# Layer norm's centring and max with zero: from VectorE to ScalarE, with the negated mean as bias

## The chip, the cores and the metric

The kernel runs on one core of a Trainium2 chip. The metric is device time in microseconds (us), the median of the runs. The core's engines are TensorE (PE; PEld is its load of the stationary operand), VectorE (DVE), ScalarE (ACT), GpSimd (POOL) and SyncE (SP, which here only issues DMAs). Each has its own queue of instructions [...].

## The reference, cut to what matters

Four graph attention layers with a residual, on x of 16 graphs, 1024 nodes and 256 features, f32:

```
for layer in 0..3:
    h = maximum(layernorm(x), 0)           # per node: (x - mean) / sqrt(var + eps), eps 1e-5
    x = x + gat_layer(h, adj, W, a)        # Wh = h @ W; masked softmax-like weights; weights @ Wh
```

The layers differ in the form of their weights (leaky ReLU, ReLU, its negative) and in what follows the sum (nothing, ELU, ELU, four heads with a norm of their own). Since the reciprocal root is positive, it may be applied after the projection: `max(x - mean, 0) @ W`, then times rstd.

## The kernel before, in words

One program, unrolled over the 16 graphs (`batch(b)`). Two streams, one for even and one for odd graphs, are written as Python generators; a small loop always advances the stream with the smaller sum of yielded costs, so that the text of the program alternates between two graphs in different layers. The instructions of an engine then stand in an order that a planner makes from this text and the dependencies. It need not be the order of the text: in the trace, L226 of a layer norm stands between L273 and L274 of another tile's finish.

`project(l, xb, pair, evict)` is the function that the diff touches. It handles two tiles of 128 nodes ("a pair"; 4 pairs x 4 layers x 16 graphs = 256 calls, called a project below):

- VectorE: `bn_stats` (L220) and `bn_aggr` (L221) for each of the two rows of tiles, mean and variance in `mv`
- VectorE L211 and GpSimd L212: `rstd`
- VectorE L226, twice: `above` = max(x - mean, 0), 128 x 256
- TensorE L230: two transposes of each `above` into the PSUM tile `turned` (named misc, 3 buffers)
- ScalarE L232: copy of `turned` to `hT` in SBUF
- TensorE L236: `projected` = hT x W, 4 matmuls for each row of tiles
- `evict`: ScalarE's exponentials (L286, L306) and a scaled copy to `V` or `h` (VectorE L290, ScalarE L288 and L307), in layer 3 also GpSimd (L309, L313, L314; L314 adds a constant to x in place)

`weigh` makes the attention weights: ScalarE copies a row from PSUM (L251), and VectorE multiplies it with the mask, 8 times 128 x 512 (L255), for each half of the target nodes. `attend` multiplies the weights with V (TensorE L338, `acc`), and a finish puts the result into x: in layer 0 on VectorE alone (L263, L264, L354), in layers 1 and 2 with the ELU (`add_elu`: VectorE L263, L264, L273, L274, ScalarE L271 `below`, GpSimd L275). In layer 3 the matmul is L414, ScalarE copies its result to `sums` (L418), TensorE transposes that (L423), and VectorE, GpSimd and ScalarE norm the heads. `load` fetches a graph to come: ScalarE squares and casts its adjacency tiles (L116, L122).

After finish(i) for even i, `attend` calls `project` of the next layer for the two rows of tiles just done, so the layer norm follows the end of the layer before, tile by tile. The tiles named `above` come from the pool `work` with 3 buffers, shared by `project` and `add_elu`; `mv` and other small tiles have 6.

Of the kernel before, what the change touches and what calls it, by code (L numbers as in the profile page):

```python
# [31 lines left out]
F32 = mybir.dt.float32  # L32
# [4 lines left out]
AF = mybir.ActivationFunctionType  # L37
ALU = mybir.AluOpType
AX = mybir.AxisListType

P = 128
# [17 lines left out]
def short_path(ctx: ExitStack, tc: tile.TileContext, ins: dict, out: bass.AP, bad: bass.AP):  # L59

    nc = tc.nc
# [72 lines left out]
    bias = const.tile([P, D], F32, name="bias")  # L134
# [11 lines left out]
    with tc.tile_pool(name="prep", bufs=2) as prep:  # L146
# [30 lines left out]
        for l, form in enumerate(forms):  # L177
            n = EXT[l] // 3
# [25 lines left out]
    small = ctx.enter_context(tc.tile_pool(name="small", bufs=6))  # L204
# [4 lines left out]
    def inverse_root(var: bass.AP, n: int, eps: float, scale: float = 1.0) -> bass.AP:  # L209
        r = small.tile([P, n], F32, name=f"rstd{n}")  # L210
        nc.vector.tensor_scalar(r, var, scale, eps, op0=ALU.mult, op1=ALU.add)  # L211
        nc.gpsimd.tensor_tensor(r, r, minus_half.to_broadcast([P, n]), op=ALU.pow)  # L212
        return r

    def project(l: int, xb: bass.AP, pair: int, evict):

        mv = small.tile([P, 2, nc.vector.BN_AGGR_DIM], F32, name="mv")
        for n in range(2):
            stats = small.tile([P, nc.vector.BN_STATS_DIM], F32, name="stats")
            nc.vector.bn_stats(stats, xb[:, 2 * pair + n, :])  # L220
            nc.vector.bn_aggr(mv[:, n, :], stats)  # L221
        rstd = inverse_root(mv[:, :, 1], 2, LN_EPS)
        turned = psum.tile([P, NK, 2 * P], F32, name="misc", bufs=3)
        for n in range(2):
            above = work.tile([P, D], F32, name="above")
            nc.vector.tensor_scalar(  # L226
                above, xb[:, 2 * pair + n, :], mv[:, n, 0:1], 0.0, op0=ALU.subtract, op1=ALU.max
            )
            for k in range(NK):
                nc.tensor.transpose(turned[:, k, ts(n, P)], above[:, ts(k, P)], ident)  # L230
        hT = wide.tile([P, NK, 2 * P], F32, name="hT")
        nc.scalar.copy(hT, turned)  # L232
        for n in range(2):
            projected = psum.tile([P, D + EXT[l]], F32, name="projected")
            for k in range(NK):
                nc.tensor.matmul(  # L236
                    projected, hT[:, k, ts(n, P)], W[l][:, k, :],
                    start=(k == 0), stop=(k == NK - 1),
                )
            evict(2 * pair + n, projected, rstd[:, n : n + 1])  # L240
# [36 lines left out]
    def batch(b: int):  # L277
# [40 lines left out]
        def attend(l: int, V: bass.AP, finish, then: int):  # L318
# [12 lines left out]
            for i in range(NI):  # L331
                t = next(weighing[1], None)
                if t:
                    yield t
                acc = psum.tile([P, HALF], F32, name="acc", bufs=3)[:, : D + 1]
                w = halves[i // NG]
                for j in range(NI):
                    nc.tensor.matmul(  # L338
                        acc, w[:, j, ts(i % NG, P)], V[:, j, : D + 1],
                        start=(j == 0), stop=(j == NI - 1),  # L340
                    )
                finish(i, acc)
                yield 3.6
                if i % 2 == 0 and i > 0:
                    project(then, xb, i // 2 - 1, following[1])
                    yield 4.0
            project(then, xb, NI // 2 - 1, following[1])
            yield 4.0
            return following[0]
# [12 lines left out]
        for pair in range(NI // 2):  # L362
            project(0, xb, pair, evict)
            yield 4.0
# [473 lines left out]
```

## Time and profile before

| | |
|---|---|
| median of 3 runs | 3343.65 us (3341.39 to 3344.26) |
| the profiled execution | 3342.89 us |
| its span, first to last instruction | 3341.3 us |
| granted TensorE clock | 0.988 of full |
| TensorE busy | 3103.0 us, 93% |
| VectorE busy | 2504.0 us, 75% |
| ScalarE busy | 974.3 us, 29% |
| GpSimd busy | 1091.2 us, 33% |

A group in the profile is a line of the kernel on one engine: how many instructions, their busy time together, the mean of one in ns, then the idle time of the engine directly before them and what ended it. The chain is followed back from the last instruction: each step to what released it, or to the instruction before it on its engine. A wait is an engine's idle time before an instruction, put down to the producer that came last.

### The profile page before, as it was taken

What the parts mean: (1) busy time and instruction counts of PE and PEld (TensorE: products, weight loads), DVE (VectorE), ACT (ScalarE), POOL (GpSimd) and SP (SyncE); (2) the same over time, 40 slices, a digit from 0 to 9 for tenths busy, and PEclk for the clock granted to TensorE, in tenths of its full rate; (3) what the DMA queues carried; (4) which work ended last, traced back from release to release, by engine and by line L of the source; (5) the groups of instructions that cost most, each with busy time, mean ns of one, the idle gap of its engine ahead of it and who ended that gap; (6) DMA issues with size and microseconds to landing.
All of it is one profiled execution on the core that took longest, in us unless ns stands there. A gap on an engine that the chain in (4) does not pass through costs nothing.

```text
span 3341.3 us, 38569 instructions
## 1 busy us (share of the span) xinstructions
PE 3103.0 (93%) x13702; PEld 2107.8 (63%) x13702; DVE 2504.0 (75%) x6140; ACT 974.3 (29%) x2081; POOL 1091.2 (33%) x1286
## 2 busy tenths in 40 slices
PE   6899999999989999899998999989999899998987
PEld 5765756657656675665756667566666666656652
DVE  5677787777778777787777877778777787777766
ACT  3423323232232322323233232332323223232121
POOL 1223324233242332424234142242323423234242
PEclk9999999999999999999999999999999999999998
DMA  4101101011010110101011010010101101000000
GB/s 115 26 4 16 32 11 40 7 17 29 13 39 8 16 29 13 38 10 16 26 16 35 10 42 4 13 35 13 39 4 17 32 13 38 7 10 13 1 13 14
DMA packets 55192, 73.19 MB, mean 22 GB/s; under 512 B 4049, under 2 KB 37969, under 8 KB 54993
## 3 DMA queue, kind: packets, MB, share of 16 engines
q0 software_dynamic: 18432, 33.56, 6.7%
q1 hardware_dynamic: 36560, 37.10, 3.5%
q8 instruction: 110, 1.80, 0.2%
q14 instruction: 90, 0.73, 0.1%
HBM read 87.43 MB, written 16.78 MB: 31 GB/s over the span
## 4 chain that ended last, share of the span: by engine, by line
DVE 45%; PE 42%; POOL 5%; ACT 4%; issue 3%; DMA 1%; SPq 0%; ACTq 0%; POOLq 0%; DVEq 0%
DVE weights L255 25%; PE acc L338 18%; PE acc L414 11%; PE projected L236 10%; DVE above L226 3%; PE misc L230 3%; DVE above L273 2%; DVE stats L220 2%; DVE above L274 2%; POOL x_b L275 2%; DVE V L290 2%; DVE y L380 1%; POOL y L379 1%; POOL rstd L212 1%; ACT below L271 1%
## 5 line engine op out<-in xcount | busy, mean ns | idle before, releaser
L338 PE MATMUL acc<-V,weights 128*128 128x257 f32 x6144 | 1454.9, 385 | 12.5 <-DVE weights L255 11.5
L338 PEld LDWEIGHTS acc<-V,weights 128*128 128x128 f32 x6144 | 1137.8, 191 | 208.9 <-DVE weights L255 47.2
L414 PE MATMUL acc<-weights,V 128*65 128x512 f32 x2048 | 914.2, 593 | 0.3 <-DVE weights L255 0.3
L255 DVE SCALAR_TENSOR_TENSOR weights<-row,ex,mask 128x512 f32<-128x512 f32 x1024 | 762.7, 784 | 2.7 <-ACT row L251 0.9
L255 DVE SCALAR_TENSOR_TENSOR weights<-row,V,mask 128x512 f32<-128x512 f32 x768 | 559.4, 776 | 53.0 <-ACT row L251 52.9
L414 PEld LDWEIGHTS acc<-weights,V 128*65 128x65 f32 x2048 | 278.7, 138 | 492.7 <-issue 474.0
L212 POOL TENSOR_TENSOR rstd<-rstd,minus_half 128x2 f32<-128x2 f32 (+1 forms) x320 | 311.3, 975 | 745.7 <-DVE rstd L211 703.2
L236 PE MATMUL projected<-W,hT 128*128 128x259 f32 (+1 forms) x2048 | 521.8, 398 | 14.8 <-ACT hT L232 11.3
L236 PEld LDWEIGHTS projected<-W,hT 128*128 128x128 f32 x2048 | 383.5, 195 | 130.1 <-ACT hT L232 60.4
L275 POOL TENSOR_TENSOR x_b<-x_b,above 128x256 f32<-128x256 f32 x256 | 227.5, 890 | 585.8 <-DVE above L274 532.5
L230 PE MATMUL misc<-ident,above 128*128 128x128 f32 x1024 | 189.1, 289 | 155.3 <-DVE above L226 108.6
L271 ACT ACTIVATE below<-acc,inv 128x256 f32<-128x256 f32 x256 | 120.0, 472 | 607.4 <-DVE inv L264 497.0
L232 ACT COPY hT<-misc 128x512 f32<-128x512 f32 x256 | 149.1, 586 | 495.8 <-PE misc L230 494.8
L230 PEld LDWEIGHTS misc<-ident,above 128*128 128x128 f32 x1024 | 113.7, 143 | 256.0 <-DVE above L226 120.3
L220 DVE BATCH_NORM_STATS2 stats<-x_b 128x6 f32<-128x256 f32 x512 | 206.7, 414 | 83.1 <-POOL x_b L275 78.9
L263 DVE TENSOR_SCALAR inv<-acc 128x1 f32<-128x1 f32 x256 | 37.3, 150 | 272.5 <-PE acc L338 272.3
L418 ACT COPY sums<-acc 65x512 f32<-65x512 f32 x128 | 74.0, 578 | 546.2 <-PE acc L414 546.1
L226 DVE TENSOR_SCALAR above<-x_b,mv 128x256 f32<-128x256 f32 x512 | 222.0, 443 | 3.8 <-POOL x_b L275 1.7
L105 POOL DMA_DIRECT2D adj_i<-in_adj_dram x128 | 77.1, 603 | 406.3 <-ACT sums L418 174.4
L290 DVE TENSOR_SCALAR V<-projected,rstd,V 128x256 f32<-128x256 f32 x256 | 134.8, 537 | 63.9 <-ACT V L286 62.9
L286 ACT ACTIVATE V<-projected,rstd 128x3 f32<-128x3 f32 x384 | 99.4, 261 | 262.0 <-PE projected L236 220.1
L314 POOL TENSOR_TENSOR x_b<-x_b,beta 128x256 f32<-128x256 f32 x128 | 117.3, 923 | 150.7 <-DVE above L226 148.6
(70 smaller groups left out, 2370.1 us busy)
## 6 DMA issues: line engine op xcount, KB each, us to landing
adj_i<-in_adj_dram POOLq DMA_DIRECT2D x128, 256.0 KB, 3.8
x_b<-in_x_dram SPq DMA_DIRECT2D x16, 1024.0 KB, 7.8
out_dram<-y SPq DMA_DIRECT2D x32, 512.0 KB, 3.8
W<-in_L_gnn_W_dram SPq DMA_DIRECT2D x3, 256.0 KB, 3.0
a_b<-in_L_gnn_a_dram SPq DMA_DIRECT2D x3, 256.0 KB, 6.4
a_b<-in_L_gnn_a_src_dram SPq DMA_DIRECT2D x1, 640.0 KB, 7.5
a_b<-in_L_gnn_a_dst_dram SPq DMA_DIRECT2D x1, 640.0 KB, 9.4
W<-in_L_gnn_W_dram SPq DMA_DIRECT2D x2, 128.0 KB, 8.9
```

The source lines that it names most:

```text
L212: nc.gpsimd.tensor_tensor(r, r, minus_half.to_broadcast([P, n]), op=ALU.pow)
L220: nc.vector.bn_stats(stats, xb[:, 2 * pair + n, :])
L226: nc.vector.tensor_scalar(above, xb[:, 2 * pair + n, :], mv[:, n, 0:1], 0.0, op0=ALU.subtract, op1=ALU.max)
L230: nc.tensor.transpose(turned[:, k, ts(n, P)], above[:, ts(k, P)], ident)
L232: nc.scalar.copy(hT, turned)
L236: nc.tensor.matmul(projected, hT[:, k, ts(n, P)], W[l][:, k, :], start=(k == 0), stop=(k == NK - 1),)
L255: nc.vector.scalar_tensor_tensor(w[:, j, :], r, c(j), mask[:, j, ts(half, HALF)], op0=op, op1=ALU.mult)
L271: nc.scalar.activation(below, acc[:, :D], AF.Exp, scale=inv)
L275: nc.gpsimd.tensor_add(xi, xi, above)
L290: nc.vector.tensor_scalar(V[:, i, :D], projected[:, :D], rstd, V[:, i, D : D + 1], op0=ALU.mult, op1=ALU.mult,)
L338: nc.tensor.matmul(acc, w[:, j, ts(i % NG, P)], V[:, j, : D + 1], start=(j == 0), stop=(j == NI - 1),)
L414: nc.tensor.matmul(accT, V3[:, j, h, :], w[:, j, :], start=(j == 0), stop=(j == NI - 1))
```

## The change

Behind the statistics of the two rows of tiles ScalarE makes `minus_mean`, 128 x 2, from both means. Then, for each row of tiles, ScalarE writes `above` as Relu(x + minus_mean) with `minus_mean`'s column as bias per partition, instead of VectorE's tensor_scalar (subtract, then max with 0). `minus_mean` is a new small tile with 6 buffers; the transposes read `above` as before. `inverse_root` stays on VectorE and GpSimd. All other lines are unchanged; the planner makes the order of each engine anew.

```diff
         rstd = inverse_root(mv[:, :, 1], 2, LN_EPS)
+        minus_mean = small.tile([P, 2], F32, name="minus_mean")
+        nc.scalar.mul(minus_mean, mv[:, :, 0], -1.0)
         turned = psum.tile([P, NK, 2 * P], F32, name="misc", bufs=3)
         for n in range(2):
             above = work.tile([P, D], F32, name="above")
-            nc.vector.tensor_scalar(
-                above, xb[:, 2 * pair + n, :], mv[:, n, 0:1], 0.0, op0=ALU.subtract, op1=ALU.max
+            nc.scalar.activation(
+                above, xb[:, 2 * pair + n, :], AF.Relu, bias=minus_mean[:, n : n + 1]
             )
```

## The prediction

> **What bounds the kernel now.** I read the page first (busy shares, the shares of the chain, the costly groups), then the sum of the waits, then the chain in order of time, then the timeline around a few layer norms.
>
> From the page, and from the chain of the whole execution, its shares by line:
>
> ```profile
> PE 3103.0 (93%) x13702; PEld 2107.8 (63%) x13702; DVE 2504.0 (75%) x6140; ACT 974.3 (29%) x2081; POOL 1091.2 (33%) x1286
> DVE 45%; PE 42%; POOL 5%; ACT 4%; issue 3%; DMA 1%; SPq 0%; ACTq 0%; POOLq 0%; DVEq 0%
> L230 PE MATMUL misc<-ident,above 128*128 128x128 f32 x1024 | 189.1, 289 | 155.3 <-DVE above L226 108.6
> L226 DVE TENSOR_SCALAR above<-x_b,mv 128x256 f32<-128x256 f32 x512 | 222.0, 443 | 3.8 <-POOL x_b L275 1.7
> ...
> by line: DVE weights L255 25.1%; PE acc L338 17.6%; PE acc L414 10.9%; PE projected L236 9.6%; DVE above L226 3.3%; PE misc L230 2.6%; issue 2.5%; DVE above L273 2.4%; DVE stats L220 2.3%; DVE above L274 2.0%; POOL x_b L275 1.7%; DVE V L290
> ```
>
> PE works 3103.0 of 3341.3 us: 238.3 us is all that any change outside PE can win. Of that idle time 155.3 us lies directly in front of the transposes L230, the readers of `above`, the tile whose maker is changed. So what decides is when `above` is ready. VectorE is the other half of the chain: 45% of it, with L226 at 3.3%, or 110 us. ScalarE is busy 29% and makes 4% of the chain.
>
> The waits, us in total, times, longest:
>
> ```profile
> PEld misc L230 <- DVE above L226: 120.3, 148, 3.5
> PE misc L230 <- DVE above L226: 108.6, 129, 3.1
> ACT sums L418 <- PE acc L414: 546.1, 97, 10.2
> ACT hT L232 <- PE misc L230: 494.8, 164, 11.9
> ACT V L286 <- PE projected L236: 220.1, 306, 3.0
> DVE weights L255 <- ACT row L251: 53.8, 26, 4.7
> ```
>
> PE stands 129 times, 0.84 us each, until VectorE has written `above`; the first-row transposes of a project carry most of it (I count 129 of the 256 projects that idle there). ScalarE's idle time is mostly standing in front of an instruction that PE has not fed yet: up to 10.2 us at `sums`.
>
> One such place in the timeline (start, length, instruction, idle time before it):
>
> ```profile
> 1228.13 0.35 DVE L226 TENSOR_SCALAR above<-x_b,mv 128x256 f32<-128x256 f32 x1
> 1228.40 0.16 DVE L211 TENSOR_SCALAR rstd<-mv 128x2 f32<-128x2 f32 x1
> ...
> 1228.54 0.20 PEld L230 LDWEIGHTS misc<-ident,above 128*128 128x128 f32 x2 [0.28 <-DVE above L226]
> ...
> 1228.73 0.68 DVE L226 TENSOR_SCALAR above<-x_b,mv 128x256 f32<-128x256 f32 x1
> ...
> 1229.47 0.44 PE L230 MATMUL misc<-ident,above 128*128 128x128 f32 x2 [0.49 <-DVE above L226]
> ```
>
> PE starts the transposes 0.06 us after the L226 that they read, with nothing else to do; VectorE has statistics and a finish of another tile between the two rows; and the second L226 takes 0.68 us instead of 0.35.
>
> [...] The trace shows one ACT_TABLE_LOAD (1283 ns, at 7.9 us) for Square, Exp and Copy together; no reload is charged. [...] L226 has median 345, mean 443, longest 1359 ns. [...]
>
> **The change, part by part.**
>
> *Removed from VectorE*: 512 L226, 222.0 us busy; VectorE goes from 2504 to about 2282 us (68%).
>
> *Added to ScalarE*: the row with an SBUF source and a pointer bias is not in the trace. [...] L116, the same form at N = 1024, [...] measures 1134, and a PSUM source with a pointer scale takes 472 (L271). I take 493, bounds 470 and 500. `minus_mean` [...] upper bound 262 (median of L286, 3 columns with a pointer). Sum 512 x 0.493 + 256 x 0.188 = 300 us; ScalarE goes to about 1275 us (38%), not a bound by itself. No DMA is issued or moved, and SP has none of this work. On POOL, L314 waits 148.6 us for L226 to have read x; that wait passes to ScalarE, and as nothing is shown waiting for L314, I charge nothing (upper bound 10 us).
>
> *On the path, first part: from the last `bn_aggr` to PE.* Before: 0.35 us, or 0.55 where L211 stands in between. After: handoff to ScalarE 0.12 (median from L264 to an idle L271), 0.188 for `minus_mean`, about 0.12 until its successor may read it (taken as the same; not in the trace, 0 at least), 0.493 for the row: 0.92 us. That is +0.37 to +0.57. The second row comes about 0.40 later (493 less an overlap of 93) where VectorE needed 0.26 to 0.28: +0.12. And `minus_mean` reads both rows' means, so the first row can no longer go ahead of the second row's statistics (414 + 171 ns). PE takes both rows' transposes 0.28 us apart in the median, so this matters only sometimes. I take +0.6 us for each of the 129 waiting projects, 77 us; bounds 48 (0.37) and 142 (1.1). Not all of it arrives: PE idles 83 us at other places (238.3 - 155.3), which shrink when PE comes later. I let two thirds through: **+51 us**.
>
> *Second part: ScalarE's queue.* Behind `minus_mean`, while it waits for VectorE, stand `hT`, `sums`, `V`, `row` and `below`, for which PE and VectorE wait. And it can itself stand behind a `sums` that PE hasn't fed. Lower bound: met busy 29% of the time for half an instruction of 0.47 us, 0.07 x 129 = 9 us. Upper: over one microsecond each, 150 us. The order on each engine is not that of the text (L226 stands between L273 and L274 in the trace) but comes from a plan, which should place most of these sensibly: **+29 us** (0.22 each).
>
> *Third part: VectorE's relief.* 110 us of the chain is L226. In about a quarter of that (my count: 69 pieces of about 260) L226 stands directly before PE's transposes, where ScalarE's work replaces it, as charged above; 83 us was mere occupation of VectorE. PE, nearly always busy, can turn little of it into time: half, **-42 us**; bounds 0 and -83.
>
> Sum +51 + 29 - 42 = **+38 us**. The profiled execution took 3342.9 us around its span of 3341.3, 0.8 below the median 3343.65 of the runs: 3342.9 + 38 = **3381 us**, +1.1%.
>
> **The rivals.**
>
> *Relief wins* (0.25). VectorE's queue is what makes `above` late (0.68 us rows, other work between rows), and an idle ScalarE writes it sooner. For it: the chain's 45% on VectorE. Against: the longer path. With relief -83, path 48 x 2/3 = 32, queue 9: -42, or **3301 us**. It decides where the added delay of a waiting project stays below about 0.3 us.
>
> *ScalarE's head of queue blocks* (0.15). `minus_mean` waits for a VectorE that is in a run of weights (8 x 0.78 us), and `hT` or `sums` behind it keep PE waiting, or it waits behind `sums`. For it: [...] the waits of 5.6 us each at `sums`. Against: 70% idle, a plan. Path 77 in full, queue 150, relief -42: +185, **3528 us**; a milder one, at half the queue's price, 3450.
>
> *Nothing lands* (0.08). The plan puts other matmuls ahead of the transposes, so that the longer path is covered: **3343 us**.
>
> **How the numbers follow.** The likeliest, 0.52, gives 3381. A measurement of this kernel can tell about 0.2% (7 us) from no change. Faster 0.25 (relief), same 0.08, slower 0.67 (0.52 + 0.15). The range 3310 to 3470 leaves out the stronger half of the two outer cases; by itself the likeliest has 3362 to 3425 (path 32 to 95, two thirds of its bounds, with queue and relief as taken).
>
> **What the profile after would show.** L226 gone from VectorE, busy there about 2282; ScalarE near 1275 with 512 rows of 0.49 and 256 of 0.19; one table load. In front of L230, idle time on PE above 155 us, put down to ScalarE; if it is below 120, the path's step is wrong and relief wins. A wait of L232 or L418's readers on ScalarE that grows tenfold (PEld for `hT` is 60 us now) would be the blocked queue. Idle before L255 for `row` above 54 us would show VectorE held by ScalarE.

## The result, and the profile after

The median went from 3343.41 to 3346.18 us (four runs each, 3341.39 to 3344.26 and 3343.14 to 3347.99): a ratio of 1.0008, interval 0.9991 to 1.0026. No change, where 3381 us and a range from 3310 to 3470 were forecast. The profiled execution took 3347.73 us, its span is 3346.1 us.

The page of the kernel after: busy times, the chain by engine, and the groups of the new rows (L224 the negation, L228 the Relu), of the transposes (L232) and of the projection (L238):

```profile
PE 3098.2 (93%) x13702; PEld 2124.8 (64%) x13702; DVE 2381.6 (71%) x5628; ACT 1235.0 (37%) x2849; POOL 1082.2 (32%) x1286
PE 54%; DVE 30%; ACT 6%; POOL 6%; issue 3%; DMA 1%; SPq 0%; POOLq 0%; ACTq 0%
L238 PE MATMUL projected<-W,hT 128*128 128x259 f32 (+1 forms) x2048 | 527.7, 402 | 36.2 <-ACT hT L234 34.8
L232 PE MATMUL misc<-ident,above 128*128 128x128 f32 x1024 | 190.6, 292 | 139.3 <-ACT above L228 138.9
L224 ACT ACTIVATE minus_mean<-mv 128x2 f32<-128x2 f32 x256 | 51.4, 202 | 526.7 <-DVE mv L221 514.3
L228 ACT ACTIVATE above<-x_b,minus_mean 128x256 f32<-128x256 f32 x512 | 235.9, 502 | 17.1 <-POOL x_b L277 4.9
```

The prices were near: 502 and 202 ns for the new rows (493 and 188 forecast, which no trace of before shows). So was the direction in which work moved: the chain passed from VectorE (45% to 30%) to TensorE (42% to 54%). But TensorE's idle time in front of the transposes did not grow. It fell from 155.3 to 139.3 us (the prediction had named above 155 as the sign that it was right, below 120 as the sign that the relief wins; neither came). What it lost came back in front of the projection, which waits for `hT`: 36.2 us after, 14.8 before, as the group of the kernel before shows:

```profile
L236 PE MATMUL projected<-W,hT 128*128 128x259 f32 (+1 forms) x2048 | 521.8, 398 | 14.8 <-ACT hT L232 11.3
```

All of TensorE's idle time, the span less its busy time, went from 238.3 to 247.9 us.

The waits of the kernel after (us in total, times, longest):

```profile
ACT minus_mean L224 <- DVE mv L221: 514.3, 186, 10.5
...
PEld misc L232 <- ACT above L228: 197.4, 165, 5.2
...
PE misc L232 <- ACT above L228: 138.9, 76, 4.8
...
PE projected L238 <- ACT hT L234: 34.8, 24, 2.7
```

TensorE stands 76 times for `above` instead of 129, but 1.8 us each time instead of 0.84: fewer and longer stops. And in 186 of 256 projects ScalarE stands at the negation until VectorE's statistics are there.

One project in the timeline of the kernel after (start, length, instruction, idle before it), and below it the busy times of the engines in four stretches around it (the column behind POOL is the granted TensorE clock):

```profile
1518.92 1.00 ACT L122 CAST mask<-misc 128x1024 uint8<-128x1024 bf16 x1
...
1519.31 0.16 DVE L221 BATCH_NORM_AGGREGATE mv<-stats 128x2 f32<-128x6 f32 x1
1519.83 0.21 ACT L224 ACTIVATE minus_mean<-mv 128x2 f32<-128x2 f32 x1
1520.13 0.91 ACT L228 ACTIVATE above<-x_b,minus_mean 128x256 f32<-128x256 f32 x2
...
1520.69 0.44 PE L232 MATMUL misc<-ident,above 128*128 128x128 f32 x2 [2.23 <-ACT above L228]
```

```profile
1517.00:1519.00 2.00, 1.46 (x7) 0.94 (x5) 2.00 (x7) 2.00 (x6) 1.31 (x2) 1.00 0.00 0
1519.00:1520.70 1.70, 0.01 (x1) 0.01 (x1) 0.59 (x5) 1.61 (x5) 1.70 (x2) 1.00 0.02 5
1520.70:1524.10 3.40, 3.40 (x14) 2.77 (x15) 1.50 (x8) 1.39 (x3) 3.14 (x4) 0.57 0.56 77
1524.10:1528.00 3.90, 3.90 (x20) 3.36 (x20) 2.82 (x8) 1.83 (x6) 1.89 (x3) 0.94 0.02 4
```

All that the prediction charged is in this picture. The statistics end at 1519.47, ScalarE is busy with a mask until 1519.92 (the queue), then come the negation and the first row, and TensorE starts 1.22 us behind the statistics after 2.23 us without work. (A busy ScalarE is not the usual case: in 218 of 256 projects the negation starts within 0.2 us of the aggregate.) Then something follows that it did not charge: for the next 3.4 us TensorE gets about half its clock (0.57 of full in the third stretch).

### The profile page after: what moved, and what is told of

It reads as the page before. It is cut to its first block, busy times and chain, and to the rows that moved or that the text cites. A ratio compares the mean times of both kernels' runs of the same rounds, so it can differ in the third digit from the quotient of the medians.

```text
span 3346.1 us, 38658 instructions
## 1 busy us (share of the span) xinstructions
PE 3098.2 (93%) x13702; PEld 2124.8 (64%) x13702; DVE 2381.6 (71%) x5628; ACT 1235.0 (37%) x2849; POOL 1082.2 (32%) x1286
## 4 chain that ended last, share of the span: by engine, by line
PE 54%; DVE 30%; ACT 6%; POOL 6%; issue 3%; DMA 1%; SPq 0%; POOLq 0%; ACTq 0%
PE acc L340 22%; DVE weights L257 19%; PE acc L416 15%; PE projected L238 11%; PE misc L232 3%; POOL rstd L212 2%; DVE above L276 2%; POOL x_b L277 1%; DVE stats L220 1%; PE misc L249 1%; DVE above L275 1%; DVE y L382 1%; ACT above L228 1%; ACT mask L122 1%; DVE y L394 1%
## 5 line engine op out<-in xcount | busy, mean ns | idle before, releaser
L257 DVE SCALAR_TENSOR_TENSOR weights<-row,V,mask 128x512 f32<-128x512 f32 x768 | 570.1, 787 | 79.3 <-ACT row L253 79.3
L238 PE MATMUL projected<-W,hT 128*128 128x259 f32 (+1 forms) x2048 | 527.7, 402 | 36.2 <-ACT hT L234 34.8
L238 PEld LDWEIGHTS projected<-W,hT 128*128 128x128 f32 x2048 | 384.2, 196 | 151.8 <-ACT hT L234 87.8
L277 POOL TENSOR_TENSOR x_b<-x_b,above 128x256 f32<-128x256 f32 x256 | 219.7, 860 | 618.5 <-DVE above L276 541.6
L232 PE MATMUL misc<-ident,above 128*128 128x128 f32 x1024 | 190.6, 292 | 139.3 <-ACT above L228 138.9
L232 PEld LDWEIGHTS misc<-ident,above 128*128 128x128 f32 x1024 | 122.8, 146 | 219.0 <-ACT above L228 197.4
L224 ACT ACTIVATE minus_mean<-mv 128x2 f32<-128x2 f32 x256 | 51.4, 202 | 526.7 <-DVE mv L221 514.3
L228 ACT ACTIVATE above<-x_b,minus_mean 128x256 f32<-128x256 f32 x512 | 235.9, 502 | 17.1 <-POOL x_b L277 4.9
```

The source lines that it names most:

```text
L228: nc.scalar.activation(above, xb[:, 2 * pair + n, :], AF.Relu, bias=minus_mean[:, n : n + 1])
L238: nc.tensor.matmul(projected, hT[:, k, ts(n, P)], W[l][:, k, :], start=(k == 0), stop=(k == NK - 1),)
L257: nc.vector.scalar_tensor_tensor(w[:, j, :], r, c(j), mask[:, j, ts(half, HALF)], op0=op, op1=ALU.mult)
L277: nc.gpsimd.tensor_add(xi, xi, above)
```

## The experiments

Each ratio is to runs of before taken beside the experiment, whose median lay between 3343.41 and 3347.6 us; so differences of absolute times between experiments are good to some 4 us. Three questions were put: what the pieces are worth, what of the path costs, and how much of any difference is the planner's order.

**The whole step away** (e1): the transposes read `xb[:, 2 * pair + n, ts(k, P)]`, and L226 is gone.

> The kernel before without the making of `above`: the transposes read x itself (centring and max with 0 are left out, the statistics and rstd stay). It prices the whole step. Theory A, relief and longer path cancel in the change: here both VectorE's work (222 us busy) and the step on the path are gone, so the time falls by the relief (about 50) and by a good part of the 155 us of PE's idle time before the transposes: 3230 to 3280 us. Theory B, the planner's order covers the step and neither relief nor path is worth anything: 3320 to 3343 us.

3272.41 us, ratio 0.9779 (0.9763 to 0.9795): 74 us is what making `above` costs in the kernel before, with the wait for the statistics in it. Theory A.

**VectorE's work given back** (e2):

```diff
             nc.scalar.activation(
                 above, xb[:, 2 * pair + n, :], AF.Relu, bias=minus_mean[:, n : n + 1]
             )
+            spare = work.tile([P, D], BF, name="spare", bufs=1)
+            nc.vector.tensor_scalar(
+                spare, xb[:, 2 * pair + n, :], mv[:, n, 0:1], 0.0, op0=ALU.subtract, op1=ALU.max
+            )
```

> The kernel after, and VectorE makes the centred rows a second time, into a bf16 tile that nobody reads: ScalarE's path as in the change, but VectorE's relief taken back. Theory A: the time rises by what the relief was worth, 40 to 60 us, to 3385 to 3405. Theory B: VectorE has room, 3340 to 3355 us.

3362.40 us, ratio 1.0047 (1.0031 to 1.0064): 16 us over after, neither the 40 of theory A nor the nothing of theory B. VectorE was busy 2551 us. TensorE's idle time did not grow (247.0 us for 247.9); its busy time did, from 3098.2 to 3115.4 us for the same matmuls (last section). Time on VectorE by itself is cheap here, in this one order; if the change's relief is larger, it lies in where the rows stood in VectorE's queue.

**ScalarE's work added to before** (e3): the same way round, `spare` made by ScalarE with `minus_mean`, and `above` by VectorE as before.

> The kernel before, and ScalarE makes the negated mean and the centred rows a second time, into a bf16 tile that nobody reads: 300 us more on ScalarE's queue, which now waits for VectorE's means, with neither the relief nor the longer path. Theory A (path and relief): 3340 to 3350 us. A blocked ScalarE queue as the cost that eats the relief: 3365 us or more. Theory B: 3340 to 3350 us.

3398.13 us, ratio 1.0145 (1.0125 to 1.0164), 52 us slower. Load on ScalarE's queue is dear even where nobody reads its result. Between the profiled executions, 58 us apart, TensorE's idle time rose by 28 us and its busy time by 30 (3132.6 for 3103.0; its time at half clock cost 69 us instead of 41, last section). The idle time before the transposes rose from 155.3 to 171.0 us, that before the projection did not rise.

**Another order of before** (e4): the line of `inverse_root` moved below the copy to `hT`.

> The kernel before, with the call of inverse_root written after the copy to hT instead of ahead of the transposes: the same instructions, another text, so another order from the planner. It shows how far a new order alone moves the time. Theory A and B: within 10 us of 3343. If it moves by 30 us or more, differences of that size between kernels here are not those of the instructions changed.

3347.89 us, ratio 1.0007 (0.9998 to 1.0016), 12 runs. This looked like proof that the order does not matter. It was not; see e14.

**A longer path** (e5):

```diff
         nc.scalar.mul(minus_mean, mv[:, :, 0], -1.0)
+        for _ in range(2):
+            turned_sign = small.tile([P, 2], F32, name="sign", bufs=12)
+            nc.scalar.mul(turned_sign, minus_mean, -1.0)
+            minus_mean = turned_sign
```

> The kernel after with the mean negated twice more on ScalarE before it is used: the path from the statistics to the transposes grows by two instructions of 0.2 us and two hand-overs, some 0.6 us for each of the 256 projects, about as much as the change itself was said to add, and ScalarE gets 100 us more work. Theory A (what the path adds reaches the end, at two thirds, and was paid back by VectorE's relief): +40 to +55 us, 3385 to 3400. Theory C (the planner puts other matmuls ahead of the transposes, so a longer path costs little): up to +15 us, 3346 to 3361.

3395.12 us, ratio 1.0154 (1.0137 to 1.0171): 49 us over after, theory A. In the traces the shortest time from the second row's aggregate to the first transpose went from 0.83 to 1.30 us. The path's length does reach the end, and the two negations' 0.2 us each in ScalarE's queue with it; the experiment does not part the two. Of the 46 us between the profiled executions, 19 are idle time of TensorE and 28 longer busy time.

**The negation on VectorE, row by row** (e6): `nc.vector.tensor_scalar_mul(minus_mean, mv[:, n, 0:1], -1.0)` inside the loop over the rows.

> The kernel after, but VectorE negates each row's mean by itself (512 small instructions), so that ScalarE does only the two Relu rows and the first row need not wait for the second row's statistics. Path shorter by some 0.2 us, for the first row by up to 0.8 us[...]. Theory A: 20 to 30 us faster than after, 3315 to 3330. Theory C: within 10 us of after, 3336 to 3356.

3341.41 us, ratio 0.9986 (0.9979 to 0.9993), 20 runs: 5 us under after, outside theory A's span and inside theory C's.

**No wait for the statistics, rows by VectorE** (e7) **and by ScalarE** (e8): the diffs are against before and against after.

```diff
-                above, xb[:, 2 * pair + n, :], mv[:, n, 0:1], 0.0, op0=ALU.subtract, op1=ALU.max
+                above, xb[:, 2 * pair + n, :], minus_half, 0.0, op0=ALU.subtract, op1=ALU.max
```

```diff
-        minus_mean = small.tile([P, 2], F32, name="minus_mean")
-        nc.scalar.mul(minus_mean, mv[:, :, 0], -1.0)
...
-                above, xb[:, 2 * pair + n, :], AF.Relu, bias=minus_mean[:, n : n + 1]
+                above, xb[:, 2 * pair + n, :], AF.Relu, bias=minus_half
```

> The kernel before with a constant in place of the mean (the centring is left out): the same instructions on the same engines, but `above` does not depend on the statistics any more. It prices the wait for the statistics alone where VectorE makes the rows. Theory A: the 155 us of idle time before the transposes shrink, 20 to 40 us faster, 3305 to 3325. Theory C: within 15 us of before, 3330 to 3350.

> The kernel after with a constant in place of the negated mean (the centring is left out, and with it the 256 negations): ScalarE makes the rows, and no longer waits for VectorE's statistics. With VectorE's relief in hand and the new wait of ScalarE for VectorE gone. Theory A: the longer path is gone and the relief stays, 40 to 60 us faster than before, 3285 to 3305. Theory C: the relief alone is worth what the second making by VectorE showed, about 16 us, 3320 to 3335.

e7: 3344.37 us, ratio 0.9996 (0.9987 to 1.0005), 12 runs. e8: 3283.54 us, ratio 0.9814 (0.9798 to 0.983). This pair is the heart of the study. On VectorE taking the dependence on the mean away wins nothing (3344.37 us, 3343.41 before): theory C, and TensorE's idle time before the transposes is no shorter than before. The author's reading, which no run tests, is that the rows stand behind the statistics in VectorE's order anyway. e8 is theory A. Between the two, with no mean in either, the move from VectorE to ScalarE wins 61 us. And from e8 to after, where only negation and mean come back, 62 to 63 us are lost. The transposes of e7, then the rows and the transposes of e8:

```profile
L230 PE MATMUL misc<-ident,above 128*128 128x128 f32 x1024 | 188.6, 291 | 158.9 <-DVE above L226 111.7
...
L226 ACT ACTIVATE above<-x_b,minus_half 128x256 f32<-128x256 f32 x512 | 244.8, 505 | 288.2 <-DVE x_b L352 173.0 <-POOL x_b L273 99.3 <-PE misc L228 12.0
L228 PE MATMUL misc<-ident,above 128*128 128x128 f32 x1024 | 185.0, 285 | 97.1 <-ACT above L226 96.2 <-DVE both L195 0.4
```

In e8 ScalarE waits almost only for x itself (272 of 288 us), and so may go ahead of the statistics, which no kernel that subtracts the mean can do. TensorE's idle time before the transposes is 97.1 us, against 158.9 in e7, 139.3 in the kernel after and 155.3 before.

**Queue or path** (e9): the constant as in e8, but `minus_mean` is still made, as in after, and read by nobody.

> The kernel after with a constant as bias (the centring is left out), but ScalarE still makes the negated mean, which nobody reads: its queue stands before the negation until VectorE's statistics are there, and the rows do not need it. Theory P (the length of the path statistics, negation, Relu, transposes costs the 62 us between after and the kernel with a constant): 3285 to 3300. Theory Q (ScalarE's queue, blocked at the negation, costs them): 3325 to 3350.

3308.25 us, ratio 0.9893 (0.9876 to 0.9909), between the theories: 25 us more than e8 for the stop of ScalarE's queue at the negation, 38 us less than after, which are the rows' wait for it. In the waits of e9:

```profile
ACT minus_mean L224 <- DVE mv L221: 270.4, 162, 5.3
...
PE misc L232 <- ACT above L228: 87.6, 81, 3.2
...
PE projected L238 <- ACT hT L234: 49.2, 37, 2.6
```

TensorE's wait for `above` is as short as in e8 (96.2), its wait for `hT`, behind the stopped queue, has risen from 22.0 to 49.2 us. So the stop of the queue shows in front of `hT`. Its 25 us are the difference of the medians; the two profiled executions are only 16 us apart, 17 us of it idle time of TensorE (211.8 us for 194.6), so the size is known to some 10 us.

**Both means negated by VectorE at once** (e10; `nc.vector.tensor_scalar_mul` in place of `nc.scalar.mul`), **one row on each engine** (e11; ScalarE makes row 0 from its own negated mean, VectorE row 1 as before), **each row with its own negation on ScalarE** (e12):

> The kernel after, with the negation of both means in one instruction on VectorE instead of ScalarE: one hand-over less on ScalarE, the rows stay coupled, VectorE gets 256 small instructions. Theory P: the path is some 0.15 us shorter, 5 to 15 us faster than after, 3331 to 3341. Theory Q: ScalarE still stands before the first Relu, 3341 to 3351.

> Of the two rows of a project ScalarE makes the first (negated mean of that row, then Relu) and VectorE the second as before. Half of VectorE's relief, and ScalarE's row, 0.9 us behind its statistics, runs beside VectorE's statistics (0.59) and row (0.35) of the second. Theory P: half the relief (about 30) with little of the longer path: 3310 to 3330 us. Theory Q: ScalarE's queue stands before the negation all the same: 3335 to 3355 us.

> The kernel after with one negation for each row on ScalarE, so that the first row no longer waits for the second row's statistics; 256 small instructions more on ScalarE. If the coupling of the two rows was a good part of the cost: 10 to 25 us faster than after, 3321 to 3336. If PE takes both rows together anyway: 3340 to 3360, the extra instructions costing as much as the first row gains.

e10: 3384.70 us, ratio 1.0119 (1.0102 to 1.0135). e11: 3381.77 us, 1.0113 (1.0096 to 1.013). e12: 3337.95 us, 0.9974 (0.9966 to 0.9983), 13 runs. e10 and e11 lie outside the spans of both theories, 38 and 36 us over after. For e10 the forecast of a shorter path was itself wrong: 0.93 us at least from the aggregate to the transposes, against 0.83. e12 is 8 us under after, between its two spans; if the two rows' coupling costs anything, it is less than what another order alone moves (below).

**The same kernels in another order** (e13 to e18): `LAG = 120.0` becomes `118.0`. The second stream starts two units of planned cost earlier; no instruction is added or removed.

> The kernel before with LAG 118 instead of 120: the same instructions, the second stream two units earlier, another order on every engine. Theory F (the forms make the differences): within 10 us of before, 3336 to 3356. Theory O (the planner's order makes them): 15 to 50 us away, to either side.

> The kernel after with LAG 118. Theory F: beside e13, within 10 us. Theory O: its distance to e13 is another than the 3 us between after and before, by 15 us or more, to either side.

> e8 (ScalarE makes the rows with a constant as bias; the centring is left out) with LAG 118. Theory F: again 60 us under e14, 3275 to 3295. Theory O: the 60 us were the order's in good part, and the distance to e14 is under 35 us.

> e10 once more as it is, with LAG 120, for one look on this chip beside e13 to e15: if its time is the kernel's own and not that of one chip or hour, 3375 to 3395.

> e10 (VectorE negates both means, ScalarE makes the rows) with LAG 118. Theory O (its order made it slow): within 15 us of e14, 3307 to 3337, at the path's length slightly under e14. Theory F: again 38 us over its after, 3350 to 3370.

> e11 (the first row on ScalarE, the second on VectorE) with LAG 118. Theory O: 3310 to 3345. Theory F: again 36 us over before, 3370 to 3395.

| kernel | LAG 120, us | LAG 118, us | ratio at 118 |
|---|---|---|---|
| before | 3343.41 | 3351.49 (e13) | 1.0015 (1.0008 to 1.0022) |
| after | 3346.18 | 3322.11 (e14) | 0.9926 (0.991 to 0.9943) |
| ScalarE, constant | 3283.54 (e8) | 3286.86 (e15) | 0.982 (0.9804 to 0.9836) |
| pair negated by VectorE | 3384.70 (e10) | 3417.38 (e17) | 1.021 (1.0193 to 1.0227) |
| one row each | 3381.77 (e11) | 3340.00 (e18) | 0.9984 (0.9978 to 0.9991) |

(e16, whose name says 118, is e10 once more at 120, beside e13 to e15: 3383.64 us in one run, so e10's time is its own.)

The kernel after moves by 24 us with its order and e11 by 42, before by 4 to 8, e8 by 3. e13, by itself, is within theory F's 10 us. e11's loss was its order's: theory O. e10's was not: it stays slow and gets slower, beyond the spans of both theories, with theory F's sign. e15 lies in theory F's span but only 35 us under e14, at the edge of theory O. e14, the change with LAG 118, is 29 us under e13, theory O, and beats before and after at 120: 0.7% faster than before. Its transposes wait less:

```profile
L232 PE MATMUL misc<-ident,above 128*128 128x128 f32 x1024 | 190.5, 291 | 98.9 <-ACT above L228 98.8
```

98.9 us instead of 139.3, with the same instructions. e9, e12 and the others were not repeated in a second order.

## Why the prediction was wrong, by its own steps

The sum was +51 for the path, +29 for ScalarE's queue, -42 for VectorE's relief. The experiments at LAG 120 have a number for each:

| step | predicted | measured | from |
|---|---|---|---|
| path | +51 | +38 | after less e9 |
| ScalarE's queue | +29 | +25 | e9 less e8 |
| relief | -42 | -61 | e8 less e7 |
| sum | +38 | +2 | after less before: +3 |

The steps of the table are differences along one row of kernels (before, e7, e8, e9, after), so that their sum must come out, but for the 1 us between before and e7. Its agreement with the result proves nothing; the single steps have to stand by themselves.

**The term that failed is the third, the relief: -42 forecast, -61 measured, and -65 at LAG 118 (e15 less e13, where VectorE's rows keep the mean).** It took 83 us of the chain as mere occupation of VectorE, of which it let half count, and wrote off the quarter that stood directly before TensorE's transposes as "replaced" by ScalarE. e2 points to the reverse weights: the occupation by itself, given back, costs 16 us. The larger part of what the move wins is that the rows need not stand in VectorE's queue: e8, with 505 ns for a row instead of 443, still cuts the idle time before the transposes from 155.3 to 97.1 us. The evidence was in the timeline shown ahead of it, two L226 0.6 us apart with other work of VectorE between, and the rival "relief wins" named it; the sum did not use it.

The costs failed too, and pushed the sum the same way, too high: +80 forecast for path and queue together, 63 measured at LAG 120 and 35 at 118 (e14 less e15). And the split has a limit. The -61 us are won by rows that may go ahead of their statistics, and the +38 us are what waiting for them takes back; in the kernel after the two act on the same transposes, and no experiment parts them there. If e2's 16 us alone are called the relief, the costs are 19 us. Either way the forecast costs were too high for what the move gave.

**The path** was right in kind, for partly wrong reasons. Its shortest length came out at 0.83 us, not 0.92: the hand-over to ScalarE takes 34 ns in the median, not 120. The delay of 0.6 us in 129 projects is 0.30 on the average of all 256; in the traces the first row's transposes start on average 5.78 us behind the second row's aggregate, 5.58 before, and the second row's 6.48 in both. That is path and relief together, and it is nearly nothing. The count of 129 waits did not survive either, as the new order has 76 longer ones. e5 confirms that a longer path, with its work on ScalarE, is paid for.

**The queue** was near (25 for 29), and e9 shows the mechanism: the stop in front of `hT`. The 25 us hold for that place: in the kernel before, the same negation and the 512 rows more on ScalarE cost 52 (e3). It is not that the negation finds ScalarE busy: it starts within 0.2 us of the aggregate in 218 of 256 projects.

**What the prediction priced at nothing**: the order. It counted the terms as if the rest stood still. With path and queue at 35 us instead of 63 under LAG 118, the zero of the result is one draw: the same change is worth -29 us beside e13. The table above is therefore good to some 25 us where `after` is in it. The result lies within the range (3310 to 3470), which the relief's rival had opened downwards; the forecast of a slower kernel was wrong. "No change" had been given 0.08, as a case of its own ("nothing lands"), and not as what two large terms of opposite sign can add up to.

**VectorE's busy time** was to fall to 2282 us and fell to 2381.6. L226's 222 us are gone, but 63 of them had overlapped with its neighbours (without L226, VectorE's busy time in the trace of before is 2345.0 us), and other rows grew by 37. Of those, 26 are in the last step of the ELU, first before, then after:

```profile
L274 DVE SCALAR_TENSOR_TENSOR above<-below,above 128x256 f32<-128x256 f32 x256 | 125.2, 492 | 1.1
...
L276 DVE SCALAR_TENSOR_TENSOR above<-below,above 128x256 f32<-128x256 f32 x256 | 150.8, 592 | 3.9
```

Like L226, L276 is stretched in some of its instructions only: median 424 ns, longest 1489. In the trace of the kernel after, 157 of the 256 have no instruction of GpSimd running beside them and take 419 ns in the mean, 426 at most; 93 have one beside them for at least half of their time and take 895. It was the same with L226 before: 145 alone took 355 ns at most, and each of the 88 longer than 600 ns had GpSimd beside it. That GpSimd's work is the cause was not tested.

**What stays open**: why e10 and e17 are slow. Their path is 0.1 us longer than after's, for which e5's rate (49 us for 0.47) would give 10 us; they lose 38 (to after) and 95 (to e14). Of that, 26 and 37 us are longer busy time of TensorE (last section). The rest is 12 us of idle time in e10, about what the rate gives, and 59 in e17, which it does not explain. Why the clock falls more often in both was not found.

## What to carry to other kernels

Here the step feeds an engine that is nearly full (TensorE, 93%), and moving it changed two large terms of opposite sign (-61 and +63 us at LAG 120). Taking its dependence away (a constant for the mean) on both engines showed their size; adding work that nobody waits for measured only a quarter of the relief (16 of 61 us). Look for an instruction's worth in what stands before it in its queue, more than in its busy time. And where a planner makes the order, repeat each kernel in a second order before believing a difference of 1%: here a shift of two units moved one kernel by 42 us and another by 3.

## What the hardware showed unasked

TensorE's granted clock fell to 0.50 of full for pieces of 3.4 us (sometimes two together) about the end of idle gaps of TensorE of mostly 2 us and more. Before, there were 18 such pieces, 82.5 us in all, so 41 us lost, if half the clock is half the work; after 24, with 50; in e17 41, with 105. One piece in each is some 18 us long and is the end of the kernel. In the kernel after, 22 of the 46 gaps over 2 us had a piece that began within 3.5 us of their end (10 of them before it), and 2 of 33 between 1 and 2 us. So a long stop can cost up to an estimated 1.7 us (half of 3.4) more than itself. Gaps of 1.9 to 3.1 us, with transposes and matmuls around them, stood at 20 of the 24 pieces. What lowers the clock was not shown.

The prediction took TensorE's work as fixed at 3103.0 us. It is not, though all these kernels have the same 13702 matmuls (us, profiled executions; idle is the span less busy):

| kernel | lost at half clock | TensorE busy | TensorE idle |
|---|---|---|---|
| before | 41 | 3103.0 | 238.3 |
| after | 50 | 3098.2 | 247.9 |
| VectorE's work given back (e2) | 65 | 3115.4 | 247.0 |
| ScalarE's work added to before (e3) | 69 | 3132.6 | 266.5 |
| longer path (e5) | 67 | 3125.8 | 266.7 |
| ScalarE, constant (e8) | 40 | 3091.0 | 194.6 |
| pair negated by VectorE (e10) | 76 | 3124.2 | 259.5 |
| after, LAG 118 (e14) | 45 | 3105.1 | 215.8 |
| pair negated, LAG 118 (e17) | 105 | 3142.4 | 274.5 |

Where more is lost at half clock the same matmuls mostly take longer; in e2 this is the whole of the loss, in e3, e5 and e10 half of it or more. From before to after the busy time fell by 5 us, so it does not explain the result, and e8's gain is mostly idle time. That the clock is the cause of the longer busy time was not tested apart.
